# Cross-attention: values weighed for 512 tokens at once, and a group's projection moved into the next group's first half

## The chip, the cores and the metric

The kernel runs on one core of one Trainium2 chip. The metric is device time in microseconds (us) of one execution, taken as the median of several runs. The profile is that of one execution; its times are counted from the first to the last instruction of the core, which is called the span.

## The reference, cut to what matters

A decoder block with causal self-attention, cross-attention and a feed-forward part is followed by a fusion block. There are B = 4 sequences of T = 1024 tokens with C = 512 channels and H = 16 heads of DH = 32. The change is in the cross-attention alone, whose keys and values come from a context of S = 64 positions:

```python
xn2 = _ln(x, g2, be2)
q = einsum('btc,hcd->bhtd', xn2, Wq_c) + bq_c      # likewise k and v, from the context
scores = einsum('bhtd,bhsd->bhts', q, k) / scale
attn = softmax(scores, axis=-1)
ca = einsum('bhts,bhsd->bhtd', attn, v)            # the weighing of the values
x = x + (ca @ W2 + b2)                             # the projection
```

## The kernel before, in words

The kernel has three phases, `self_attention`, `cross_attention` (L973) and `feed_forward` (L1255). Work is written as steps with a cost each, and `run` (L106) weaves several streams of steps together by the shares of their costs that are left. The instructions of one engine are then put into a fixed order when the program is built, by a scheduler that works from the order of writing and from its own estimate of when each instruction can start. On the chip every engine goes through its own list strictly in order.

Cross-attention works on eight groups of 512 tokens (`groups`, two to a sequence). For a group, `self_end` (L1036) makes what comes first: the self-attention's projection (`adds`, tile `po_x`, L1071), its sum with x and the norm, the transposes of the normed tokens (`turn` at L1056, tile `tpn_x`), and the queries (`query` at L1067, tile `pq_x`), which land in the pair of tiles `qT`, a high and a low part. Products that need near full precision are done as three products of such parts; in the profile all of them are on L102, told apart by tile. `cross` (L1087) then does the attention of the group, in eight halves: four blocks `j` of 128 tokens, times two halves of the heads.

- `scores` (L1094): six products of 256 columns into one of two `sc` banks, the least value of each head by VectorE (L1104), then the exponentials. For one half of the heads VectorE subtracts (L1113) and ScalarE does one wide exponential (L1114); for the other ScalarE does eight narrow ones (L1110) straight from the bank. GpSimd multiplies by the inverse sums (L1118).
- `turn` (L1121): four transposes into the one `tp` bank (L1126, tile `tpp_c`), copied by ScalarE to `pT` (L1128), 128 tokens wide.
- `weigh` (L1131): four fp32 products of 64 weight columns by 128 tokens (L1139, tile `av_c`), alternately into the upper and lower 64 partitions. After the second half `split` (L71) cuts the bank into the two parts `ca` (ScalarE L74, VectorE L75).
- `project` (L1153): twelve products of 512 columns (tile `po_c`), the sum with x (L1150), and the store of x to DRAM (L1151).

The order within `cross` is that of L1166: each round writes the scores of one half, the transposes of the half two rounds back and the weighing of the half three rounds back; every second round has the projection of a block whose `ca` is complete. The loop at L1226 runs these steps of group k beside one long stream: the `adds` of group k+2, then the queries of k+1, then the transposes of k+2, with the loads for k+3 strewn in.

Of the eight PSUM banks three belong to `mm` (`po_x`, `tpn_x`, `pq_x`), one to `tp`, two to `av` (`av_c` and `po_c`) and two to `sc`. The x tiles have twelve slots, three groups. A load into a slot waits for the store of the x tile that was there (both on SyncE's queue).

Of the kernel before, what the change touches and what calls it, by code (L numbers as in the profile page):

```python
# [10 lines left out]
F32 = mybir.dt.float32  # L11
FR = mybir.dt.float32r
# [6 lines left out]
P = 128  # L19
B, T, C, H = 4, 1024, 512, 16  # L20
DH = C // H
S = 64
FF = 4 * C
NC = C // P
# [28 lines left out]
def decoder_then_fusion(ctx: ExitStack, tc: tile.TileContext, x, ctxT, cols, rows,  # L53
# [61 lines left out]
    def run(*streams, speed=None, sooner=None):  # L115


        speed = [v for v, s in zip(speed or [1.0] * len(streams), streams) if s]
        sooner = [v for v, s in zip(sooner or [0] * len(streams), streams) if s]
        streams = [s for s in streams if s]  # L120
        left = [sum(t for t, _ in s) or 1 for s in streams]
        total, at = list(left), [0] * len(streams)
        while any(i < len(s) for i, s in zip(at, streams)):
            k = min((k for k in range(len(streams)) if at[k] < len(streams[k])),
                    key=lambda k: (1 - left[k] / total[k]) / speed[k])
            t, f = streams[k][at[k]]
            if sooner[k]:
                with tc.high_priority(offset=sooner[k]):
                    f()
            else:  # L130
                f()
            left[k] -= t
            at[k] += 1

    def behind(*engines):

# [316 lines left out]
    def self_attention(ph):  # L453
# [62 lines left out]
        def front(b, n):  # L516
# [20 lines left out]
                split(parts[0][:, c, :], parts[1][:, c, :], tp, f"{uid}_{c}")  # L537

            return [(0, lambda j=j: load(j)) for j in range(NJ)], [(TG, lambda c=c: turn(c)) for c in range(NC)]

        def among(steps, extra):

            out, n = list(steps), len(extra)
            for i in reversed(range(n)):
                out.insert((i + 1) * len(steps) // (n + 1), extra[i])
            return out

        def tiles_of(b, g):

# [423 lines left out]
    def cross_attention(ph):  # L973
# [27 lines left out]
        ptp = ph.enter_context(tc.tile_pool(name="pt_x", reuse_waits="tile", bufs=3))  # L1001
        big = ph.enter_context(tc.tile_pool(name="big_x", reuse_waits="tile", bufs=1))

        def parts_of(name, uid, bufs=1):
            pool = {"qT": big, "sa": sap, "xn": xnp}[name]
            return [pool.tile([P, NC, TG], FR, tag=f"{name}{k}", name=f"{name}{k}_{uid}", bufs=bufs)
                    for k in range(2)]

        sas, state = {}, {}

        def self_parts(b, n):

            uid = f"x{b}_{n}"

            def begin():
                if b == B - 1:
                    for step in invert_steps(b, n, nc.sync):
                        step()

                sas[b, n] = parts_of("qT", uid, 2) if Z["sa1"] and (b, n) == groups[1] else parts_of("sa", uid)  # L1020

            def divide(g):
                inv = avp.tile([P, TG], F32, tag="inv", name=f"inv_{uid}_{g}")
                src = inv_dram[b, n].rearrange("(g r) t -> g r t", r=HG)
                for r in range(HG):
                    nc.sync.dma_start(inv[r * DH : (r + 1) * DH],
                                      src[g, r : r + 1].to_broadcast([DH, TG]))
                av = avp.tile([P, TG], F32, tag="sav", name=f"sav_{uid}_{g}")
                nc.sync.dma_start(av, av_dram[b, n, g])
                nc.gpsimd.tensor_tensor(av, av, inv, ALU.mult)  # L1030
                sa = sas[b, n]
                split_biased(sa[0][:, g, :], sa[1][:, g, :], av, col("bv_s", g))

            return [(0, begin)] + [(1, lambda g=g: divide(g)) for g in range(NC)]

        def self_end(b, n):  # L1036
# [18 lines left out]

            def turn(c):  # L1056
                if c == 0:
                    held["xn"], held["q"] = parts_of("xn", uid), parts_of("qT", uid, 2)
                    state[b, n] = xs, held["q"]
                xn = held["xn"]  # L1060
                tp = psum(f"tpn_{uid}_{c}")
                for j, t in enumerate(hs):
                    nc.tensor.transpose(tp[:, j * P : (j + 1) * P], t[:, c * P : (c + 1) * P], ident)
                nc.scalar.activation(tp, tp, AF.Identity, bias=col("be2", c), scale=col("g2", c))
                split(xn[0][:, c, :], xn[1][:, c, :], tp, f"{uid}_{c}")

            def query(ps, g):  # L1067
                q = held["q"]
                split_biased(q[0][:, g, :], q[1][:, g, :], ps, nbq[:, NC + g : NC + g + 1])

# [16 lines left out]
        def cross(b, n):  # L1087
# [6 lines left out]
            def scores(j, half):  # L1094
# [9 lines left out]
                nc.vector.tensor_reduce(top, sc, AX.X, ALU.min)  # L1104
                pr = ptp.tile([P, HH, S], F32, tag="p", name=f"p_{uid}")
                den = small.tile([P, HH], F32, tag="denc", name=f"den_{uid}", bufs=2)
                if half:
                    nc.vector.tensor_scalar(top, top, QSCALE, None, ALU.mult)
                    for h in range(HH):
                        nc.scalar.activation(pr[:, h], sc[:, h], AF.Exp, scale=-QSCALE,  # L1110
                                             bias=top[:, h : h + 1], accum_out=den[:, h : h + 1])
                else:
                    nc.vector.tensor_tensor(pr, sc, top.unsqueeze(2).to_broadcast([P, HH, S]), ALU.subtract)  # L1113
                    nc.scalar.activation(pr, pr, AF.Exp, scale=-QSCALE)  # L1114
                    nc.vector.tensor_reduce(den, pr, AX.X, ALU.add)
# [5 lines left out]
            def turn(j, half):  # L1121
                uid = f"c{b}_{n * NJ + j}_{half}"
                pr = held.pop((j, half)).rearrange("p h s -> p (h s)")
                tp = ps_tp.tile([P, TG], F32, tag="tp", name=f"tpp_{uid}")
                for k in range(4):
                    nc.tensor.transpose(tp[:, k * P : (k + 1) * P], pr[:, k * P : (k + 1) * P], ident)  # L1126
                pT = ptp.tile([P, 4, P], F32, tag="pT", name=f"pT_{uid}", bufs=2)
                nc.scalar.copy(pT.rearrange("p k q -> p (k q)"), tp)  # L1128
                held["pT", j, half] = pT

            def weigh(j, half):  # L1131
                uid = f"c{b}_{n * NJ + j}_{half}"
                if half == 0:
                    held["av", j] = ps_av.tile([P, TG], F32, tag="av", name=f"av_{uid}")
                av, pT = held["av", j], held["pT", j, half]
                for k in range(4)[::-1]:
                    m = half * 4 + k
                    r = (m % 2) * 2 * DH
                    nc.tensor.matmul(av[r : r + 2 * DH, (m // 2) * P : (m // 2 + 1) * P],  # L1139
                                     vbd[:, b, m, :], pT[:, k, :], start=True, stop=True)  # L1140
                if half:
                    ca = [ptp.tile([P, NC, P], FR, tag=f"ca{k}", name=f"ca{k}_{uid}", bufs=2)
                          for k in range(2)]
                    flat = [t.rearrange("p c q -> p (c q)") for t in ca]
                    split(flat[0], flat[1], av, uid)
                    held["ca", j] = ca

            def added(ps, j):
                i = n * NJ + j
# [2 lines left out]

            def project(j):  # L1153
                return product_steps(lambda: ps_av.tile([P, C], F32, tag="av", name=f"po_c{b}_{n * NJ + j}"),
                                     lambda: held["ca", j], lambda: w2,
                                     lambda a, c: a[:, c, :], lambda w, c: w[:, c, :], C,
                                     lambda ps: added(ps, j))

            def biased(j):
# [2 lines left out]

            steps = [(0, lambda: load_context(b + 1))] if n == 0 and b < B - 1 else []
            steps += [(0, lambda j=j: biased(j)) for j in range(NJ)]
            halves = [(j, h) for j in range(NJ) for h in range(2)]
            for k in range(len(halves) + 5):  # L1166
                if k < len(halves):
                    steps.append((3 * C, lambda at=halves[k]: scores(*at)))
                if 0 <= k - 2 < len(halves):
                    steps.append((2 * C, lambda at=halves[k - 2]: turn(*at)))  # L1170
                if 0 <= k - 3 < len(halves):
                    steps.append((2 * C, lambda at=halves[k - 3]: weigh(*at)))
                if 0 <= k - 5 and (k - 5) % 2 == 1:
                    steps += project((k - 6) // 2)
            return steps

        ends = [self_end(*at) for at in groups] + [([], [], [], [])] * 3
        run(ends[0][0] + ends[0][1])
# [1 line left out]
        if Z["a2"] >= 3:  # L1180
# [2 lines left out]

        kbd = [[wts.tile([P, NC, HG * S], FR, tag=f"kbd{k}_{i}", name=f"kbd{k}_{i}") for k in range(2)]
               for i in range(2)]
        vbd = wts.tile([P, B, H // 2, 2 * DH], F32, tag="vbd", name="vbd")

        def load_context(b):
            eng = nc.sync if b else nc.scalar
            for k, t in enumerate(kbd[b % 2]):  # L1190
                eng.dma_start(raw(t), kbd_dram[k, b])
            eng.dma_start(vbd[:, b], vbd_dram[:, b])

        gate = ExitStack()
        k = Z["a2k"]
# [25 lines left out]
        else:  # L1221
            load_w2()
            with gate:
                run(ends[2][0])
            run(ends[1][2])
        for k, at in enumerate(groups):  # L1226

            later = list(ends[k + 1][3]) + ends[k + 2][2]
            for i, step in enumerate(ends[k + 3][0]):
                later.insert(2 * i, step)  # L1230
            steps = cross(*at)
            if k == 0 and Z["w2l"]:
                steps.insert(Z["w2l"], (0, load_w2))
            run(steps, ends[k + 2][1] + later, speed=(1.5,1.0))

# [569 lines left out]
```

## Time and profile before

| | |
|---|---|
| median of three runs | 2153.99 us (2148.6 to 2155.89) |
| the profiled execution | 2153.24 us, span 2151.5 us |
| TensorE, VectorE, ScalarE, GpSimd busy | 96%, 67%, 45%, 56% of the span |
| granted TensorE clock, mean | 0.983 |
| cross-attention's scores, first and last start | 959.2 to 1320.0 us |
| its projections, last start | 1341.3 us |

Times in the tables of the profile are busy times of an engine. An engine's next instruction can begin before the last one's recorded end, since the engines overlap the tail of one with the head of the next; where the text speaks of a pitch, it is the time from one start to the next. An fp32 product of this kernel leaves two records, so 256 products of `av_c` are 512 records.

### The profile page before, as it was taken

The numbers are of one execution on the slowest core, as the hardware profiler recorded it, in microseconds if no ns is written. First come the engines' busy times: TensorE is split into PE (matmuls) and PEld (weight loads), VectorE is DVE, ScalarE is ACT, GpSimd is POOL, SyncE is SP. The second block draws the span as 40 slices with busy tenths as digits, with TensorE's granted clock in tenths as the row PEclk, the third lists the DMA queues.
The fourth block names the chain that finished last, engine by engine and source line by source line (L and its number), as shares of the span: only waits on it lengthen the run. The fifth ranks groups of instructions, "written<-read, shape, count | busy, mean of one in ns | idle before, by whom it ended". The sixth has DMA issues, their size and how long they took to land.

```text
span 2151.5 us, 34750 instructions
## 1 busy us (share of the span) xinstructions
PE 2064.3 (96%) x11544; PEld 1568.7 (73%) x11544; DVE 1452.1 (67%) x3134; ACT 967.5 (45%) x2180; POOL 1210.7 (56%) x1257
## 2 busy tenths in 40 slices
PE   6999998999999989989999999999999999999997
PEld 5766676667667756457888887788788888888885
DVE  6587757665755587567676776877667846865667
ACT  3365555555565545435555557433322422232222
POOL 3288878888788877774555543512343524433323
PEclk9999999999999998999999999999999999999998
DMA  8866767677666567662323122965576457655631
GB/s 245 258 186 168 218 203 216 182 243 219 190 174 186 158 171 213 206 204 79 99 84 103 50 79 86 332 210 170 182 238 198 166 175 237 207 175 171 220 113 39
DMA packets 241321, 379.36 MB, mean 176 GB/s; under 512 B 35948, under 2 KB 104284, under 8 KB 239094
## 3 DMA queue, kind: packets, MB, share of 16 engines
q1 hardware_dynamic: 215532, 348.32, 52.4%
q10 hardware_dynamic: 25610, 28.83, 4.4%
q8 instruction: 92, 1.51, 0.3%
q14 instruction: 87, 0.71, 0.1%
HBM read 251.71 MB, written 124.81 MB: 175 GB/s over the span
## 4 chain that ended last, share of the span: by engine, by line
PE 76%; DMA 7%; DVE 7%; POOL 4%; issue 2%; ACT 1%; SPq 1%; ACTq 0%; DVEq 0%; POOLq 0%
PE acc L1495 15%; PE ph L1473 14%; PE st L755 5%; PE s L692 5%; PE av L785 5%; PE po_c L102 4%; PE pq_x L102 3%; PE pk L102 3%; PE pv L102 3%; PE pg_o L102 3%; PE po_x L102 3%; PE pq L102 3%; POOL pT L809 2%; PE sc_c L87 2%; PE av_c L1139 1%
## 5 line engine op out<-in xcount | busy, mean ns | idle before, releaser
L809 POOL TENSOR_TENSOR pT<-pT,pT 128x256 f32<-128x256 f32 (+3 forms) x369 | 551.6, 1514 | 106.0 <-PE av L785 97.1
L760 ACT ACTIVATE pT<-st 128x512 f32<-128x512 f32 (+2 forms) x640 | 322.3, 559 | 171.2 <-PE st L755 122.9
L1495 PE MATMUL acc<-wf,hs 128*128 128x512 f32 x1536 | 392.1, 393 | 0.9 <-DVE y L1507 0.9
L1495 PEld LDWEIGHTS acc<-wf,hs 128*128 128x128 f32 x1536 | 285.8, 188 | 63.1 <-ACT inT L74 1.3
L699 DVE CUSTOM_DVE_ANT_0 s<-s,mask 128x128 f32<-128x128 f32 (+3 forms) x512 | 244.5, 504 | 99.6 <-PE s L692 97.1
L692 PE MATMUL s<-ks,qs 96*128 96x512 f32 (+3 forms) x768 | 230.2, 371 | 23.0 <-DMA qs<-qd 7.3
L702 DVE TENSOR_REDUCE top<-s 128x1 f32<-128x512 f32 x256 | 171.9, 684 | 104.4 <-PE s L692 103.9
L755 PE MATMUL st<-qs,ks 98*128 98x256 f32 (+2 forms) x888 | 227.8, 340 | 4.7 <-ACT pT L760 2.0
L1473 PE MATMUL ph<-inT,wp 128*128 128x512 f32 x768 | 205.3, 396 | 3.1 <-DVE p L1431 1.2
L755 PEld LDWEIGHTS st<-qs,ks 98*128 98x128 f32 x888 | 149.4, 192 | 63.7 <-issue 20.2
L692 PEld LDWEIGHTS s<-ks,qs 96*128 96x128 f32 x768 | 135.6, 194 | 81.0 <-issue 17.0
L1473 PEld LDWEIGHTS ph<-inT,wp 128*128 128x128 f32 x768 | 143.9, 189 | 36.6 <-DVE gp_o L1568 1.8
L785 PE MATMUL av<-pT,v 128*32 128x512 f32 (+3 forms) x1776 | 155.1, 454 | 4.1 <-POOL pT L768 4.1
L1473 PE MATMUL ph<-inX,wp 128*128 128x512 f32 x576 | 151.4, 395 | 1.1 <-DVE inX L75 1.1
L768 POOL TENSOR_SCALAR_AFFINE_SELECT pT<-pT 128x256 f32<-128x256 f32 x256 | 103.7, 421 | 73.6 <-ACT pT L760 73.1
L1473 PEld LDWEIGHTS ph<-inX,wp 128*128 128x128 f32 x576 | 108.4, 189 | 25.2 <-issue 1.3
L1542 POOL TENSOR_TENSOR y<-y,row_bf 128x512 f32<-128x512 f32 x32 | 41.6, 1304 | 132.6 <-DMA y<-x 72.1
L1481 ACT ACTIVATE hs<-ph 128x512 fp32r<-128x512 f32 x64 | 38.3, 599 | 172.2 <-DVE ph L1431 99.4
L102 PE MATMUL pk<-xn_s,wk 128*128 128x512 f32 x384 | 106.1, 412 | 4.9 <-DVE top L702 3.0
L102 PE MATMUL pv<-wv,xn_s 128*128 128x256 f32 x768 | 108.1, 286 | 2.5 <-DVE least L699 1.6
L102 PEld LDWEIGHTS pv<-wv,xn_s 128*128 128x128 f32 x768 | 102.1, 192 | 11.4 <-DVE top L699 2.9
L1118 POOL TENSOR_TENSOR p_c<-p_c,inv_c 128x512 f32<-128x512 f32 x64 | 68.4, 1069 | 73.9 <-DVE inv_c L1117 58.6
(262 smaller groups left out, 3907.8 us busy)
## 6 DMA issues: line engine op xcount, KB each, us to landing
wp<-wpd SPq DMA_DIRECT2D x168, 256.0 KB
ks<-kd SPq DMA_DIRECT2D x96, 256.0 KB
qs<-qd SPq DMA_DIRECT2D x96, 256.0 KB
wf<-w2fd SPq DMA_DIRECT2D x48, 512.0 KB
kd<-k SPq DMA_DIRECT2D x64, 256.0 KB
qd<-q SPq DMA_DIRECT2D x120, 128.0 KB
wpd<-wp SPq DMA_DIRECT2D x56, 256.0 KB
x<-in_x SPq DMA_DIRECT2D x32, 256.0 KB
```

What stands on the lines that cost most here:

```text
L102: nc.tensor.matmul(held["ps"], a_at(a()[i], c), b_at(b()[j], c), start=not bias and c == 0 and k == 0, stop=c == NC - 1 and k == 2)
L692: nc.tensor.matmul(part, q_at[u][:KS, r, j * P : (j + 1) * P], k_at[u, m][:KS, r, : part.shape[-1]], start=True, stop=True)
L699: nc.vector.tensor_tensor_reduce(part, part, mask[:, TG - part.shape[-1] :], 1.0, TOP, ALU.add, ALU.min, dst)
L702: nc.vector.tensor_reduce(dst, part, AX.X, ALU.min)
L755: nc.tensor.matmul(st[:, i], k_at[u, kb // NJ][:KM, r + i, (kb % NJ) * P : (kb % NJ + 1) * P], q_at[u][:KM, r + i, c0:], start=True, stop= ...
L760: nc.scalar.activation(held[kb][(r + i) // 2][:, at : at + k, c0:], st[:, i : i + k], AF.Exp, scale=-QSCALE)
L768: nc.gpsimd.affine_select(out=t, in_=t, compare_op=ALU.is_ge, fill=0.0, base=0, pattern=[[0, 2], [1, P]], channel_multiplier=-1)
L785: return nc.tensor.matmul(held["av"][r * DH : (r + 1) * DH, c0:], v_at[b, g][:, kb, r * DH : (r + 1) * DH], held[kb][r // 2][:, r % 2, c0: ...
L809: eng.tensor_tensor(t[:, :, c0:], t[:, :, c0:], p[:, :, c0:], ALU.add)
L1118: nc.gpsimd.tensor_tensor(pr, pr, inv.unsqueeze(2).to_broadcast([P, HH, S]), ALU.mult)
L1473: nc.tensor.matmul(ps, w[:, q, c], x[:, r, c], start=c == 0 and m == 0, stop=c == HC - 1 and m == 2)
L1495: mm = nc.tensor.matmul(accs[j], hidden[b, n, f][:, q, j * P : (j + 1) * P], w2s[b, f][:, r], start=begins and m == 0, stop=ends and m == 2)
```

## The change

`weigh` is now called once for each of the four blocks `c` of 128 channels, after the scores and transposes of all four token blocks, and weighs 512 tokens at a time: two fp32 products of 64 weight columns by 512 tokens, into one whole `av` bank, which is split at once into channel block `c` of `ca`. So there are 64 products of `av_c` in place of 256. The splits, the copies, the exponentials and the transposes stay as many as they were, and each of the same size; a copy now writes four strips of 128 into a `pT` that is 512 wide.

The halves run over all four token blocks of one half of the heads, then of the other. Which path the exponentials take goes by the token block and no longer by the half. `ca` lies in the room of the group's queries, which the scores have finished with by then. The room is one of two, taken in turn by the groups.

`cross` returns two lists, its own steps and its projection (`sums`). The loop runs the first half of group k's steps, with the projection of group k-1 strewn among them, beside the `adds` of k+2; then the second half beside the queries of k+1, the transposes of k+2 and the loads for k+3. The last group's projection comes at the end by itself. The context's block-diagonal values `vbd` have two buffers in place of one for each sequence.

```diff
-                pT = ptp.tile([P, 4, P], F32, tag="pT", name=f"pT_{uid}", bufs=2)
-                nc.scalar.copy(pT.rearrange("p k q -> p (k q)"), tp)
-                held["pT", j, half] = pT
+                if j == 0:
+                    held["pT", half] = ptp.tile([P, 4, TG], F32, tag="pT", name=f"pT_{uid}", bufs=2)
+                nc.scalar.copy(held["pT", half][:, :, j * P : (j + 1) * P], tp.rearrange("p (k q) -> p k q", k=4))
 
-            def weigh(j, half):
-                uid = f"c{b}_{n * NJ + j}_{half}"
-                if half == 0:
-                    held["av", j] = ps_av.tile([P, TG], F32, tag="av", name=f"av_{uid}")
-                av, pT = held["av", j], held["pT", j, half]
-                for k in range(4)[::-1]:
-                    m = half * 4 + k
-                    r = (m % 2) * 2 * DH
-                    nc.tensor.matmul(av[r : r + 2 * DH, (m // 2) * P : (m // 2 + 1) * P],
-                                     vbd[:, b, m, :], pT[:, k, :], start=True, stop=True)
-                if half:
-                    ca = [ptp.tile([P, NC, P], FR, tag=f"ca{k}", name=f"ca{k}_{uid}", bufs=2)
-                          for k in range(2)]
-                    flat = [t.rearrange("p c q -> p (c q)") for t in ca]
-                    split(flat[0], flat[1], av, uid)
-                    held["ca", j] = ca
+            def weigh(c):
+                if c == 0:
+                    held["ca"] = room_of(b, n, f"ca{b}_{n}")
+                av = ps_av.tile([P, TG], F32, tag="av", name=f"av_c{b}_{n}_{c}")
+                for k in range(2)[::-1]:
+                    m = 2 * c + k
+                    nc.tensor.matmul(av[k * 2 * DH : (k + 1) * 2 * DH], vbd[b][:, m, :],
+                                     held["pT", m // 4][:, m % 4, :], start=True, stop=True)
+                ca = held["ca"]
+                split(ca[0][:, c, :], ca[1][:, c, :], av, f"ca{b}_{n}_{c}")
...
-            halves = [(j, h) for j in range(NJ) for h in range(2)]
-            for k in range(len(halves) + 5):
+            halves = [(j, h) for h in range(2) for j in range(NJ)]
+            for k in range(len(halves) + 2):
                 if k < len(halves):
                     steps.append((3 * C, lambda at=halves[k]: scores(*at)))
                 if 0 <= k - 2 < len(halves):
                     steps.append((2 * C, lambda at=halves[k - 2]: turn(*at)))
-                if 0 <= k - 3 < len(halves):
-                    steps.append((2 * C, lambda at=halves[k - 3]: weigh(*at)))
-                if 0 <= k - 5 and (k - 5) % 2 == 1:
-                    steps += project((k - 6) // 2)
-            return steps
+            steps += [(4 * C, lambda c=c: weigh(c)) for c in range(NC)]
+            sums = []
+            for j in range(NJ):
+                sums += project(j)
+            return steps, sums
...
+        sums = []
         for k, at in enumerate(groups):
-            later = list(ends[k + 1][3]) + ends[k + 2][2]
+            steps, next_sums = cross(*at)
+            half = len(steps) // 2
+            run(among(steps[:half], sums), ends[k + 2][1])
+            ahead = list(ends[k + 1][3]) + ends[k + 2][2]
             for i, step in enumerate(ends[k + 3][0]):
-                later.insert(2 * i, step)
-            steps = cross(*at)
-            if k == 0 and Z["w2l"]:
-                steps.insert(Z["w2l"], (0, load_w2))
-            run(steps, ends[k + 2][1] + later, speed=(1.5,1.0))
+                ahead.insert(2 * i, step)
+            run(steps[half:], ahead)
+            sums = next_sums
+        run(sums)
```

## The prediction, as put on record before the run

> **What bounds the kernel now.** I read the page first, then busy time by stretches of 10 us through cross-attention, then the groups of instructions in that window, then the timeline of single products.
>
> ```profile
> PE 2064.3 (96%) x11544; PEld 1568.7 (73%) x11544; DVE 1452.1 (67%) x3134; ACT 967.5 (45%) x2180; POOL 1210.7 (56%) x1257
> PEclk9999999999999998999999999999999999999998
> ```
>
> TensorE leads, but a share of the whole span says nothing of one stage. The stretches do (columns: time, then busy us of PE, PEld, DVE, ACT, POOL, clock, DMA share, GB/s):
>
> ```profile
> 1060.00:1070.00 10.00, 10.00 (x74) 8.36 (x70) 9.04 (x16) 9.29 (x29) 2.58 (x3) 1.00 0.22 79
> 1070.00:1080.00 10.00, 10.00 (x59) 8.35 (x59) 5.37 (x12) 2.57 (x12) 5.14 (x6) 1.00 0.18 54
> ...
> 1290.00:1300.00 10.00, 8.44 (x67) 6.50 (x64) 10.00 (x22) 7.62 (x33) 2.85 (x3) 1.00 0.47 181
> 1300.00:1310.00 10.00, 10.00 (x67) 8.23 (x66) 5.49 (x13) 7.24 (x34) 2.85 (x3) 1.00 0.17 63
> 1310.00:1320.00 10.00, 9.51 (x74) 7.51 (x73) 7.94 (x16) 6.63 (x31) 3.42 (x4) 1.00 0.13 46
> 1320.00:1330.00 10.00, 8.37 (x54) 6.47 (x53) 3.37 (x9) 6.05 (x29) 3.13 (x3) 1.00 0.08 28
> ...
> 1340.00:1350.00 10.00, 7.25 (x25) 4.88 (x24) 8.62 (x14) 7.06 (x15) 6.50 (x7) 0.76 0.76 244
> ```
>
> From 970 to 1286 us PE has no gap worth naming: there, every product taken away is time saved, so long as nothing else becomes late. From 1286 to 1342, in the last two groups, PE idles 4 of 56 us. So the question is what PE saves, and whether ACT and DVE, nearly full in some stretches already, still serve it in time.
>
> **PE's saving.** The products that change, and their wide neighbour of the same kind (fp32, few weight columns, 512 tokens), in the timeline:
>
> ```profile
> 1042.43 0.27 PE L1126 MATMUL tpp_c<-ident,p_c 128*128 128x128 f32 x1
> 1042.63 0.66 PE L1139 MATMUL av_c<-pT_c,vbd 128*64 128x128 f32 x8
> 1043.22 0.50 PE L102 MATMUL pq_x<-xn_x,wqc 128*128 128x512 f32 x1
> ```
> ```profile
> 506.24 1.06 PE L822 MATMUL den<-pT,ones 128*32 128x512 f32 x8
> 507.24 0.45 PE L755 MATMUL st<-qs,ks 98*128 98x384 f32 x1
> ```
>
> Before, a half takes 1043.22 - 1042.63 = 0.59 us for eight records, in four waves of two side by side (records start 6 ns apart, waves 0.11 to 0.16 apart). Entry costs as well: the last transpose to `av_c` is 0.20 us, where to a weight product it is 0.03, so 0.17 more. That is 0.76 us x 64 halves = 48.6 us. After, a channel block is two waves of 512; the `den` waves start at 506.243 and 506.696, the next product at 507.24, and further waves of this kind follow after 0.43. The instruction order of the changed program puts two blocks together each time: 0.45 + 2 x 0.43 + 0.54 + 0.17 = 2.0 us, 16 times = 32 us. Saving 16.6 us. Bounds: if two 64-column products did not run side by side at 512 tokens, waves would be 8 instead of 4, 16 x 4 x 0.43 = 27 us more, a loss of 11; the pairs 6 ns apart speak against that, and I take 16.6.
>
> Not all of it lies in the dense part. I cut at the end of the last query product (PE row of `pq_x`: last start 1286.3, so 1286.5). Up to there the order has 49 of 64 halves before and 12 of 16 double blocks after: 37.2 - 24.0 = 13.2 us saved; but two halves' scores and transposes (0.72 + 0.36 us each) come in front of the cut now, which are 2.2. So **-11 us at the cut** if PE stays dense.
>
> **What costs nothing.** Copies (64), splits (32 + 32), exponentials and loads are as many and as big; the order shows PE alone with fewer. The `pT` copy writes strips of 128; its row is 0.60 us by element count, bounds 0 to +0.1 us a copy off the path. The room: scores have finished with the queries before `ca` is written, and the next queries for it come after the projection; cover over 10 us each, so 0. `vbd` in two buffers: its load waits for a group finished long before, 0.
>
> The moved projection also moves the store of x, which SyncE's queue must do before the load of x for group k+3, since there are twelve slots. The chain of waits has this once: x sum 0.70, store 2.05, load 2.73, GpSimd's b1 1.04 us, then a sum of 0.69 again: 7.2 us from the end of a projection until a `po_x` bank is free, and loads behind it on SyncE wait as well. With three `mm` banks the fourth `po_x` needs it; in the new order 10.8 us of PE work (three projections and a `po_x`) lie between. Hidden by 3.6 us; if GpSimd and DVE are each two instructions late, the cover is gone and each group pays 0 to 2 us. I take 0.
>
> **The seams.** Before, the transposes `tpn_x` of the next group lie among projections, which have their own two banks. After, the projections are elsewhere, and in each of six seams the order is: scores, `tpp_c`, `tpn_x`, three more scores, three `tpp_c`, with nothing else PE could do until the first `po_x`. ACT's pitch when busy, from its timeline:
>
> ```profile
> 1319.22 0.31 ACT L1110 ACTIVATE p_c<-sc_c,top_c 128x64 f32<-128x64 f32 x1
> 1319.41 0.21 ACT L1110 ACTIVATION_READ_ACCUMULATOR p_c<-sc_c,top_c 128x1 f32 x1
> 1319.51 0.32 ACT L1110 ACTIVATE p_c<-sc_c,top_c 128x64 f32<-128x64 f32 x1
> ```
>
> So eight narrow exponentials take 8 x 0.29 = 2.3 us, not the 4.5 of the busy sums; likewise pitch 0.48 for a `pT` copy or a cast, 0.68 for the `tpn_x` activation, 0.52 for a wide exponential, 0.57 for a query. In the worst seam (first group of the second sequence, second half) PE, after the score that waits for the last narrow exponential, has 0.72 + 0.72 + 0.36 + 0.45 = 2.25 us until `tpp_c` of the fourth block, which needs the bank emptied. ACT's list up to that copy: query 0.57, copy 0.48, two activations 1.36, exponential 0.52, cast 0.48, copy 0.60 = 4.0. PE waits 1.75 us; then the next score waits for a subtraction on DVE queued behind that transpose, 0.35; and the score before came 0.4 late. 2.5 us. Counted the same way the other five give 0.5, 1.0, 1.3, 1.3 and 1.7: 8.3 in all, and 0.3 each for the way from engine to engine: **10 us**. Bounds: 0 (before, PE waits nowhere there) and 27 (with the rows' whole durations in place of pitches the worst seam is 5.3, on average 4.5).
>
> **The end.** From the cut to the last projection, before: 1341.5 - 1286.5 = 55.0 us. After, PE has 43.8 us of work there (9 halves' scores 6.5, 12 sets of transposes 4.3, 4 double blocks 8.0, 8 projections 21.9, feed-forward's transposes 3.1). The last projections wait for the whole group now, four in a row. Followed link by link, ACT's and DVE's lists leave PE waiting 2.1 + 2.9 + 0.9 in the first ten us, then 1.7 and 2.6 around the last scores, and about 3 in engine-to-engine steps: 57, so **+2**. Bounds: 48 (projections cover all but the last softmax) and 62.
>
> **Sum.** 2153.2 - 11 + 10 + 2 = 2154.2 against the profiled execution; that lies 0.8 under the median of the runs shown, so I say 2155.
>
> One rule of the Trainium skill speaks against the change. The row first: after waits in 1340 to 1350, none over 1.6 us, the clock is 0.76, while in 1290 to 1300 and 1320 to 1330, with 1.6 us idle in each, it stays 1.00. "TensorE: Matmul & The Clock Gate", section "What's actually happening", has the clock halve after an idle window of about 3.4 us; by that no seam would trip it, and the sum stays. By the row of 1340 a seam that idles a quarter of its ten us might, and would run some 4 us at half speed, an estimate of 2 us a seam, 12 in all. No row shows which holds for the seams.
>
> **Rivals.**
> *ACT keeps up.* Seams cost nothing, as before 1286 now, and the end is as long as it was: 2153 - 11 = 2142. For it: over a group ACT's pitches sum to some 27 us of 46. Against: 10.5 of them fall within the 10.8 us of PE work of the worst seam.
> *The seams starve PE.* A price of 4 us a seam (24) and an end of 60 (+5): 2153 - 11 + 29 = 2171, slower. For it: PE waits in line order, the single `tp` bank makes each set of transposes wait for ACT, and p has three buffers. It decides from where seams and end together pass 18 us. Against: pitches, not durations, rule ACT in the row above.
> *The pairs do not run side by side:* 2155 + 27 = 2182; little stands for it.
>
> **How the numbers follow.** Gain given back at the seams, time within 0.3% of before (6.5 us, about what a measurement of this kernel can tell from no change): 0.37. ACT keeps up, faster: 0.27. Seams starve PE, slower: 0.33; no pairs: 0.03, slower too. The range reaches down to the second case with a shorter end (2138) and up past 2171 to an end at its bound (2173).
>
> **What would show it.** `av_c` as 128 records in waves of two 0.43 apart; PE waits at `tpp_c`, `sc_c` and `tpn_x` for ACT and DVE, some 10 us in all, in six places between 1000 and 1280; the cut about 1 us earlier than 1286.5; the end some 57 us. Wrong if PE's gaps there stay under 3 us or go over 20, if the clock drops in seams, or if `po_x` is seen waiting for x.

## The result, and the profile after

The changed kernel takes 2165.34 us (median of 6 runs, 2161.41 to 2171.03), the kernel before beside it 2151.84 us (6 runs): a ratio of 1.0063, 95% interval 1.0044 to 1.0082, so 0.6% slower. The forecast was 2155, no measurable change. The time lies inside the stated range of 2138 to 2173, but that range took in the rivals as well. What came is the rival in which the seams starve PE, at a price between its own and the forecast's.

The profiled execution of after is the fastest of the six, 2161.41 us (span 2159.7), only 8.2 above the profiled one of before. The two can't be compared end to end: the first score product starts at 953.1 us after and at 959.2 before, with the same work ahead of it, and over all builds of this study that start lies between 953 and 964. So I measure each trace over the **stage**, from its first `sc_c` to the first product of the feed-forward part (`ph`): 385.0 us before, 398.5 after. These 13.5 us are as many as lie between the medians; with one trace of each kernel, an agreement that close is partly luck.

Busy time and clock row on the page of after:

```profile
PE 2055.0 (95%) x11160; PEld 1549.9 (72%) x11160; DVE 1448.1 (67%) x3134; ACT 964.9 (45%) x2180; POOL 1213.7 (56%) x1257
...
PEclk9999999999999999999999999999999999999999
```

PE is 9 us less busy, with 384 fewer records (192 products), and yet the kernel is slower: PE waits. (The clock row shows nothing: a slice of it is 54 us wide.) The stretches of after (columns as before):

```profile
1060.00:1070.00 10.00, 10.00 (x47) 8.17 (x46) 1.66 (x3) 2.12 (x12) 1.92 (x2) 1.00 0.23 79
...
1090.00:1100.00 10.00, 6.71 (x43) 5.62 (x41) 8.35 (x13) 4.87 (x20) 6.93 (x7) 1.00 0.28 80
1100.00:1110.00 10.00, 9.26 (x48) 7.67 (x50) 6.68 (x15) 9.75 (x31) 2.09 (x2) 0.83 0.00 1
...
1300.00:1310.00 10.00, 7.09 (x26) 3.82 (x27) 6.52 (x17) 4.80 (x21) 3.13 (x3) 0.66 0.41 157
...
1340.00:1350.00 10.00, 10.00 (x46) 8.21 (x45) 5.09 (x8) 1.94 (x4) 4.49 (x5) 1.00 0.39 132
```

Read the first line against the next two. At 1060 PE is full while the softmax engines have little to do (DVE 1.66, ACT 2.12 us): projections run there that need no softmax. At 1090 PE starves, and at 1100 its clock is down as well. What PE waited for within the stage (line, releaser: us in all, times, longest), the first four lines:

```profile
PE sc_c L87 <- ACT p_c L1115: 6.7, 4, 3.5
PE tpn_x L1065 <- DVE q_qx L80: 4.0, 4, 2.1
PE sc_c L87 <- DVE p_c L1118: 4.0, 3, 2.6
PE tpp_c L1131 <- ACT pT_c L1134: 3.0, 4, 1.4
```

All lines of this view come to 24 us; in before they come to 5.8, the first being:

```profile
PE po_c L102 <- DVE ca_c L75: 2.7, 4, 1.4
```

The longest wait stands in the seam I had called the worst, in the first group of the second sequence. On PE's timeline:

```profile
1096.00 0.80 PE L1065 MATMUL tpn_x<-ident,xh_x 128*128 128x128 f32 x3
1100.33 2.34 PE L87 MATMUL sc_c<-kbd,q_qx 128*128 128x256 f32 x12 [3.52 <-ACT p_c L1115]
1102.46 1.06 PE L1131 MATMUL tpp_c<-ident,p_c 128*128 128x128 f32 x4
```

And on the timelines of GpSimd, VectorE and ScalarE, the instructions that lead to it:

```profile
1094.46 0.55 POOL L179 TENSOR_TENSOR rstd_x<-rstd_x,neg_half 128x1 f32<-128x1 f32 x1
1094.98 1.05 POOL L1123 TENSOR_TENSOR p_c<-p_c,inv_c 128x512 f32<-128x512 f32 x1
1096.39 1.27 POOL L1160 TENSOR_TENSOR x_x<-x_x,row_b 128x512 f32<-128x512 f32 x1 [0.36 <-DVE xh_x L185]
```
```profile
1095.05 1.26 DVE L185 TENSOR_SCALAR xh_x<-x_x,mv_x,rstd_x 128x512 f32<-128x512 f32 x1 [1.05 <-POOL rstd_x L179]
1096.23 0.68 DVE L75 TENSOR_TENSOR q_ca<-av_c,q_ca 128x512 fp32r<-128x512 f32 x1
1096.83 0.85 DVE L1113 TENSOR_SCALAR top_c<-top_c 128x8 f32<-128x8 f32 x1
```
```profile
1097.80 0.31 ACT L1115 ACTIVATE p_c<-sc_c,top_c 128x64 f32<-128x64 f32 x1 [4.00 <-DVE top_c L1113]
```

The brackets are read backwards. PE waits for a score bank, which eight narrow exponentials on ACT must empty. ACT stood idle 4.00 us before them, for a scaled maximum on DVE. DVE had that queued behind a normalisation of x, which waited 1.05 us for GpSimd's `rstd`, and behind a split. The exponentials then take their 2.3 us, as I had counted. Two instructions of DVE's list also ran long: the normalisation 1.26 us, where the median of its kind in this trace is 0.55, and the scaled maximum 0.85, where it is 0.17. GpSimd was at work both times, and each ended within 0.3 us after an instruction of GpSimd. The trace of before has about as many long ones, so the change did not bring them, and no run tests why they come. The profile names only the last link of such a chain.

The weighing itself became what was worked out: eight records in 1111.39 - 1109.52 = 1.87 us.

```profile
1109.52 1.94 PE L1143 MATMUL av_c<-pT_c,vbd 128*64 128x512 f32 x8
1111.39 0.66 PE L1131 MATMUL tpp_c<-ident,p_c 128*128 128x128 f32 x4
```

### The profile page after: what moved, and what is told of

Its sections match the earlier page's. It is cut to its first block, busy times and chain, and to the rows that moved or that the text cites. A ratio compares the mean times of both kernels' runs of the same rounds, so it can differ in the third digit from the quotient of the medians.

```text
span 2159.7 us, 33950 instructions
## 1 busy us (share of the span) xinstructions
PE 2055.0 (95%) x11160; PEld 1549.9 (72%) x11160; DVE 1448.1 (67%) x3134; ACT 964.9 (45%) x2180; POOL 1213.7 (56%) x1257
## 3 DMA queue, kind: packets, MB, share of 16 engines
q8 instruction: 89, 1.46, 0.3%
## 4 chain that ended last, share of the span: by engine, by line
PE 73%; DVE 9%; DMA 8%; POOL 4%; ACT 3%; issue 2%; SPq 1%; DVEq 0%; ACTq 0%; POOLq 0%
PE acc L1501 15%; PE ph L1479 14%; PE s L692 5%; PE st L755 5%; PE av L785 5%; PE pk L102 4%; PE pq L102 3%; PE pv L102 3%; PE po_c L102 3%; PE pg_o L102 3%; PE po_x L102 3%; POOL pT L809 2%; PE den L822 1%; PE pq_x L102 1%; PE sc_c L87 1%
```

## The experiments

**Theory.** PE's saving is real. But a group's twelve wide products (four output projections, four self-attention projections, four query products) need nothing of the group's own softmax any more. The planner (the scheduler that fixes each engine's order when the program is built) may spend them early, and what is left of the softmax stands bare. Before, the output projections waited for their own token blocks, so the data itself spread them. **Rivals:** the wide weighing is itself dear; the softmax lists are too long in any order; the end of the stage or the banks are the cause.

"Five groups" below is the time from the 9th to the 49th of the 64 sets of transposes `tpp_c` in the trace. Ratios are to the kernel before as it ran beside each run, with 95% intervals; each kernel is described below. The last two columns come from one trace each, and the five groups hold a slightly different number of records in each order (720 wide ones in paced, 727 in before, 738 in after).

| kernel | ratio | stage, us | five groups, us |
|---|---|---|---|
| before | 1 | 385.0 | 253.0 |
| after | 1.0063 [1.0044, 1.0082] | 398.5 | 262.5 |
| narrow products in after's order | 1.0047 [1.0029, 1.0065] | 395.7 | 263.9 |
| two query products held back | 1.0058 [1.0038, 1.0078] | 395.9 | 267.5 |
| paced | 1.0003 [0.9988, 1.0018] | 385.3 | 243.7 |
| last group in pairs | 1.0072 [1.0053, 1.0091] | 399.7 | 264.5 |
| paced, narrow products | 1.0013 [0.9993, 1.0033] | 391.1 | 245.7 |
| paced, both ends | 1.0006 [0.9989, 1.0023] | 385.6 | 245.1 |
| paced, both ends, pairs | 1.0017 [0.9998, 1.0036] | 384.2 | 245.9 |
| wide exponentials in after | 1.0048 [1.0031, 1.0064] | 393.0 | 260.2 |
| paced, first group | 0.9987 [0.9968, 1.0007] | 380.9 | 246.1 |
| paced, first group, pairs | 0.9993 [0.9973, 1.0013] | 381.4 | 246.3 |
| paced, first group, shifted | 0.9992 [0.9975, 1.0008] | 383.3 | 243.2 |
| three score banks in after | 1.0102 [1.0071, 1.0133] | 400.8 | 262.1 |

**1. Narrow products in after's order.**

```diff
-                for k in range(2)[::-1]:
-                    m = 2 * c + k
-                    nc.tensor.matmul(av[k * 2 * DH : (k + 1) * 2 * DH], vbd[b][:, m, :],
-                                     held["pT", m // 4][:, m % 4, :], start=True, stop=True)
+                for j in range(NJ):
+                    for k in range(2)[::-1]:
+                        m, at = 2 * c + k, slice(j * P, (j + 1) * P)
+                        nc.tensor.matmul(av[k * 2 * DH : (k + 1) * 2 * DH, at], vbd[b][:, m, :],
+                                         held["pT", m // 4][:, m % 4, at], start=True, stop=True)
```

> The changed kernel, but the values are weighed in products of 128 tokens again, at the same places: 512 records of av_c in place of 128, all else as it was. Theory (TensorE's saving is real, and bare softmax stretches without projections eat it): the products cost 0.59 us a half again instead of 0.43 a wave of 512, and up to 0.17 us for each more change of mode, so TensorE has 8 to 17 us more; some of that falls into the bare stretches, where TensorE waits anyway, so the time rises by 5 to 15 us over the changed kernel (2170 to 2180), and against the kernel before the move alone costs 18 to 28 us. Rival 1 (the wide products or the copies and splits around them are themselves what is dear): the time falls back towards the kernel before, 2152 to 2160. Rival 2 (TensorE does not bound cross-attention any more, the softmax lists do throughout): no change, 2163 to 2167.

Measured: 2161.11 us, no slower than after; my 2170 to 2180 was missed, and neither rival's range was met. In the trace the `av_c` products take 14 us more (46.1 in place of 31.9, from start to next start), but PE's gaps up to the last query product fall from 15.7 to 7.0: a narrow product needs only its own token block, so the planner put pieces into the bare stretches. The run doesn't tell the rivals apart; it shows what a filler there is worth.

**2. Two query products held back.** The third and fourth query product of the next group may be issued only behind two transpose sets of this group's second half. With them the transposes of the tokens after are written beside the next group's first half:

```diff
+            for i, (t, f) in enumerate(kept):
+                kept[i] = (t, lambda f=f, at=(1, 2)[i // NC]: after_turn(at, f))
```

> The changed kernel with only the order of issue changed: of the next group's four query products, the third and the fourth are put behind the second and third of a group's last four transpose sets, so that 5.2 us of projection work stands inside each seam; the work is the same. Theory (the seams starve TensorE because the planner has spent all projections before them): the seams' waits of TensorE fall from some 15 us to under 7, and with the clock that drops behind them the time falls by 8 to 15 us (2150 to 2157), unless a new bare stretch forms earlier in the second half, where these products came from; then by 3 to 8. Rival (ActE's and VectorE's lists are as long as the stretch, so what fills TensorE does not shorten it): the time stays within 3 us of 2165 and the waits stand elsewhere.

Measured: 2163.96 us, five groups 267.5. Nothing won: PE's gaps within the five groups are 13.4 us, where after has 11.4. The stall of 3.52 us at 1100 is gone, but others stand elsewhere, 1.71 us at 1051, 2.75 at 1205 and 2.37 at 1261. The time is in the rival's range and misses the theory's, with its "new bare stretch" too (3 to 8 us less). That products taken from one stretch left another bare is my reading, not shown; the next run decides.

**3. Paced.** Every wide product is put behind one of the group's eight transpose sets (c output, x self-attention, q query). The edit fixes the places of the transposes of x, the weighings and the loads as well, so it tests the order as a whole; the work is unchanged:

```diff
+        ORDER = [[('c', 0)], [('c', 1), ('c', 2)], [('c', 3)], [('x', 0), ('q', 0)], [('x', 1)], [('q', 1), ('x', 2)], [('q', 2)], [('x', 3), ('q', 3)]]
...
+                with tc.issue_after(latest["turn", groups[k], i]):
+                    for kind, n in ORDER[i]:
+                        for _, f in product(kind, k, n):
+                            f()
```

> The changed kernel with all twelve wide products of a group (four output projections, four self-attention projections, four query products) put one or two behind each of the group's eight transpose sets, so that none can be issued early; the work is the same. Theory (clustered softmax work without cover costs about 21 us, of which 11 were won by the wide products): cross-attention up to the last query product gets dense as before the change, and the time falls by 12 to 21 us, to 2144 to 2153; the end stays 59 us long. Rival (the softmax lists are too long in any order, or the moved projection's store and load chain holds the next group): the time stays at 2160 to 2168, with TensorE waiting for ACT and DVE or for x as much as now.

Measured: 2151.48 us, 0.6% under after: order alone gives back what the change cost, and its interval lies clear of that of after. Five groups take 243.7 us, 18.8 less than after and 9.3 less than before, and PE has no gap in them. Stretches of this kernel:

```profile
970.00:980.00 10.00, 8.39 (x32) 6.43 (x30) 4.00 (x9) 7.05 (x35) 4.18 (x4) 0.59 0.00 1
1090.00:1100.00 10.00, 10.00 (x55) 8.52 (x54) 5.61 (x13) 5.12 (x21) 4.51 (x7) 1.00 0.01 2
1100.00:1110.00 10.00, 10.00 (x46) 6.40 (x45) 8.49 (x17) 6.17 (x23) 4.43 (x6) 1.00 0.17 53
```

The two lines at 1090 and 1100 stand beside those of after above: PE full, DVE and ACT at an even 5 to 8.5 us. The lists are not too long; they were badly timed. But the line at 970 shows a hole at the start, with the clock at 0.59, where before and after have none, and the end (49th transpose set to `ph`) takes 83.3 us in place of 67.7 before and 78.0 after. Against before nothing is won overall.

**4. The last group in pairs of token blocks.**

```diff
+            halves = [(j, h) for j0 in range(0, NJ, 2 if last else NJ)
+                      for h in range(2) for j in range(j0, j0 + (2 if last else NJ))]
```

> The changed kernel, where the last group alone takes its blocks of 128 tokens in two pairs: both halves of the first pair, its values weighed over 256 tokens, then the second pair, so that the first two of its projections can run beside the second pair's softmax. Theory (the end grew from 55 to 59 us because all four last projections wait for the whole group): the end shrinks by 4 to 8 us to 51 to 55, and the time falls by 4 to 8 us to 2157 to 2161; the seams are untouched. Rival (the end is set by the softmax lists, not by where the projections stand): the end stays within 1.5 us of 59 and the time within 2 us of 2165.

Measured: 2167.06 us; from the last query product to the last projection 57.6 us in place of 59.4. The rival holds, to within 0.1 us of its bound on the time: the end is not set by where the projections stand alone.

**5. Paced, narrow products** (the edits of 3 and 1 together).

> The paced order, with the values weighed in products of 128 tokens again (512 records of av_c). Theory (TensorE's saving is real and worth its full size where projections cover the softmax; in the first run with narrow products it was hidden, since the narrow products of a token block can start earlier and filled the bare stretches): here, where TensorE has no gaps over five groups, the time rises by 8 to 17 us over the paced kernel (2151.5), to 2160 to 2168, and five groups take 5 to 10 us more than its 243.7. Rival (wide products save nothing, because something beside TensorE paces the groups): within 3 us of 2151.5.

Measured: 2152.77 us, five groups 2.0 us longer. The time is in the rival's range, but not for the rival's reason: nothing beside TensorE paces the groups, whose gaps are 0.4 us here. My size was off as well, and this is the most useful miss. The two kernels' `av_c`, narrow first:

```profile
1098.20 1.53 PE L1145 MATMUL av_c<-pT_c,vbd 128*64 128x128 f32 x24
1099.66 0.66 PE L1131 MATMUL tpp_c<-ident,p_c 128*128 128x128 f32 x4
```
```profile
1086.56 1.94 PE L1144 MATMUL av_c<-pT_c,vbd 128*64 128x512 f32 x8
1088.43 0.86 PE L87 MATMUL sc_c<-kbd,q_qx 128*128 128x256 f32 x5
```

Twenty-four narrow records take 1.46 us, which makes 1.95 for 32. Where 32 stand in one run, three times in this trace, they take 1.90. Eight wide ones, the same work, take 1.87. So in one unbroken run the width is worth 0.03 to 0.08 us a double block, 0.5 to 1.3 us in all. But the planner breaks the narrow ones up: `av_c` stands in 65 runs in before, 42 here and 20 in paced. With what each entry costs beyond the usual pitch, PE spends 48.9, 40.7 and 34.3 us on it. So 8.2 of the 14.6 us that paced saves come without the width, from many token blocks weighed in one go with fewer entries from other kinds of product. The other 6.4 come with the wide product, mostly because it can't be broken up. (The profiled execution took 2165.27 us, 12.5 above this kernel's median, with a lowered clock at the start; its stage is not to be leaned on.)

**6 and 7. Both ends, without and with pairs.** The first two self-attention projections ahead of the first transposes, and other lists for the first and the last two groups (those of run 6; run 7 has two of the last group's own projections in `LAST`):

```diff
+        FIRST = [[('x', 2)], [('x', 3)], [('q', 0)], [('q', 1)], [], [('q', 2)], [], [('q', 3)]]
+        SIXTH = [[('c', 0)], [('c', 1)], [('c', 2)], [('c', 3)], [('q', 0)], [('q', 1)], [('q', 2)], [('q', 3)]]
+        LAST = [[('c', 0)], [], [('c', 1)], [], [('c', 2)], [], [('c', 3)], []]
```

> The paced order, and beside it other orders for the first and the last two groups, where the pacing left TensorE without work: in the first group the first two self-attention projections come ahead of the first transposes, in the seventh one product goes behind each transpose set, in the last the four projections of the group before go behind every other set. Theory (what the paced kernel lacks against a gain is at its two ends: 7 us of idle time and a clock of 0.74 to 0.91 between 950 and 990, and some 8 us of idle time from 1250 on): the hole at the start goes and the time falls by 6 to 12 us under the paced kernel, to 2140 to 2146, faster than the kernel before. Rival (the start and the end cost the same in any order, because the first and the last softmax have nothing to hide behind): 2149 to 2154.

> As the run before, and the last group in two pairs of token blocks (values weighed over 256 tokens), so that two of its own projections run beside the second pair's softmax. Theory (the last projections waiting for the whole group cost some 4 us at the end): 2 to 6 us under the run before. Rival (ACT and DVE set the end; in the changed kernel's own order the pairs gained nothing): within 2 us of it.

Measured: 2153.09 and 2153.80 us. The rivals hold. The start (first score to 9th transpose set) went from 58.3 to 49.9 and 48.6 us as expected, and the end from 83.3 to 90.6 and 89.7: given back. The largest wait there in the kernel without pairs:

```profile
1266.85 2.49 PE L87 MATMUL sc_c<-kbd,q_qx 128*128 128x256 f32 x12 [3.84 <-ACT p_c L1115]
```

One filler a set, spread thin where the seventh group begins, makes a seam of the same kind again; with the old lists there, run 9 has an end of 84.8.

**8. Wide exponentials in after.**

```diff
-                if j % 2:
+                if False:
```

> The changed kernel, with the exponentials of every block taken in the wide form (subtraction on VectorE, one activation of 512, a sum on VectorE), where it takes every other block in eight narrow activations on ScalarE. ScalarE has 1.8 us less for each of 32 blocks, VectorE some 0.5 to 1 us more. Theory A (in the bare stretches TensorE waits for ScalarE's list, the narrow exponentials above all, as my prediction's seam count has it): the waits of sc_c for the narrow exponentials go and the time falls by 4 to 10 us, to 2155 to 2161. Theory B (the narrow exponentials only stand at the end of a chain that begins on VectorE and GpSimd: the maximum waits behind a normalisation that waits for GpSimd's rstd): the waits move to VectorE and the time stays or rises, 2164 to 2175.

Measured: 2163.42 us, between the ranges of the two theories and, within the intervals, not to be told from after. With an estimated 32 x 1.8 us taken off ACT, the waits for the narrow exponentials (6.7 us) go, and those for DVE's subtraction rise from 4.0 to 7.0. The first line now reads:

```profile
PE sc_c L87 <- DVE p_c L1118: 7.0, 7, 2.2
```

So ScalarE's list, on which my seam count rested, is not the main cause. In the trace the stage is 5.5 us shorter, so it may have a part.

**9 to 11. First group only; the same with pairs; the first with the last query product shifted into the next group** (the first two with FIRST as in 6, the second with the last group's blocks in pairs as in 4; for the third, `ORDER` and FIRST are changed so that q3 stands behind the next group's first set, and the transposes of x stand one set later).

> The paced order with only the first group's order changed as in the run with both ends (two self-attention projections ahead of the first transposes, then one product behind a set); the last two groups are as in the paced kernel. Theory (in the run with both ends, the start took 49.9 us in place of 58.3 for the same work, and the end lost as much again, 90.6 in place of 83.3, since one product a set left a bare stretch of 3.8 us where the seventh group begins): start and end are separate, so the time falls by 5 to 9 us under the paced kernel, to 2143 to 2147, faster than the kernel before. Rival (whatever is won early is lost again at the end, because the last softmax of the chain has a time of its own): 2150 to 2154.

> As the run before, and the last group in two pairs of token blocks, with the projections of the group before behind its first four transpose sets and two of its own behind the sixth and seventh. Theory (projections at the end wait for the whole group): 2 to 5 us under the run before, 2139 to 2144. Rival (the pairs did nothing in the changed kernel's order, and 0.7 us more in this one): within 2 us of it.

> The paced order, the first group as in the two runs before, and in every group the last query product moved from behind the eighth transpose set to behind the first of the next group, and the transposes of the next tokens one set later, so that each group's beginning (two scores, two weighings, four transposes of x) has a product of its own to cover it. Theory (bare stretches cost wherever they stand, and the paced kernel's and its successor's last one stands where the seventh group begins): the stall of 3.8 us there goes, 2 to 5 us under the run with only the first group changed. Rival (the list of VectorE is full in that stretch, 10.0 of 10 us, so that a product only moves the wait): within 2 us of it.

Measured: 2151.07, 2151.01 and 2151.47 us, ratios 0.9987, 0.9993 and 0.9992. All three are in their rivals' ranges. The stage of the first is 380.9 us, 4.4 under paced and 4.1 under before, less than the 5 to 9 expected, and in the medians it is not to be told from either: of 8.3 us won at the start, 3.9 are lost further on. Pairs and shift add nothing. No version of this study is shown to be faster than the kernel before.

**12. Three score banks in after** (two in place of three for `po_x`, `pq_x` and `tpn_x`).

```diff
-        ps_mm = ph.enter_context(tc.tile_pool(name="ps_mm_x", reuse_waits="tile", bufs=3, space=PSUM))
+        ps_mm = ph.enter_context(tc.tile_pool(name="ps_mm_x", reuse_waits="tile", bufs=2, space=PSUM))
...
-        ps_sc = ph.enter_context(tc.tile_pool(name="ps_sc_x", reuse_waits="tile", bufs=2, space=PSUM))
+        ps_sc = ph.enter_context(tc.tile_pool(name="ps_sc_x", reuse_waits="tile", bufs=3, space=PSUM))
```

> The changed kernel with three PSUM banks for scores in place of two, and two in place of three for the products before the softmax (po_x, pq_x and the transposes of x). Most of what TensorE waits for in the changed kernel are score banks: sc_c for the narrow exponentials 6.7 us, for the subtraction 4.0, for the maximum 1.7. Theory A (ScalarE's and VectorE's lists in the bare stretches are long, and a bank more only lets TensorE run 0.72 us further ahead once in each stretch): 0 to 5 us less, 2160 to 2165, or more time if the two other banks become short. Theory B (the bound is the two banks, not the lists): the 12 us of sc_c waits go and the time falls by 8 us or more, under 2157.

Measured: ratio 1.0102, with an interval that overlaps that of after. PE's waits at `sc_c` fall from 12.4 to 5.4 us, and others take their place, the first two lines being:

```profile
PE av_c L1143 <- ACT pT_c L1134: 4.5, 5, 1.4
PE ph L1479 <- DVE t L1413: 3.6, 1, 3.6
```

The stage is 2.3 us longer, and the feed-forward part 5.2 (from `ph` to PE's last product 799.3 in place of 794.1), which the planner orders anew as well. Up to the last projection the stage is 1.3 us shorter. So the 12 us of theory B do not come; but the run also took a bank from three other tiles, so what a score bank alone is worth it does not show.

## Why the prediction held in its range and missed in its middle

- **What bounds the kernel:** right. PE sets the pace; a product taken away is time saved where PE is dense (run 3).
- **PE's saving, 16.6 us:** near in size. On `av_c` and its entries PE spends 48.9 us before (48.6 in the forecast) and 34.1 after (32), so 14.8 are saved. Five eighths of the forecast are 10.4; paced has 9.3 in five groups, of which some 0.9 is the other mix of records. The side-by-side pairs hold too. But I credited the 512 columns with it, and by run 5 over half comes from weighing in one go.
- **What costs nothing:** right. No `po_x` waits for x, and the room and `vbd` cost nothing visible.
- **The seams, +10 us: the step that failed.** From the first score to the last query product the trace went from 327.0 to 337.2 us, where -11 + 10 stood. With the saving as predicted, the price is some 21 us. PE's gaps in this part rose from 1.7 to 15.7 us; the clock, below, adds up to 3.4; 2 to 4 us I can't assign. The places were right, even the worst one, but not the chain: I followed ACT's list up to the `pT` copy, as if every other engine delivered in time. The `pT` copy is 1.2 us of the waits in this part, score banks are 7.5 and the splits of the queries 4.0. In the seams at 1100, 1152 and 1204 ACT stood idle for 4.00, 2.27 and 2.48 us for a scaled maximum of DVE, whose list had itself waited 1.05, 0.72 and 0.43 us for GpSimd's `rstd`. At 998, where PE waited 2.09 us for a split, ACT's own list stood before it, as I had counted. I had also assumed a calm clock; that it drops in seams was one of my signs of being wrong, and in two it did.
- **The end, 57 us:** 59.4. Direction right, 2.4 too little; a score at 1303.5 waited 2.62 us for a subtraction on DVE, and the clock in 1300 to 1310 is 0.66. The step from the last projection to `ph` became 1.1 us shorter. In sum 10.2 + 4.4 - 1.1 = 13.5, the loss. That the time is still inside the range is due to its width, not to the price of the seams.
- **The clock rule of the Trainium skill** ("TensorE: Matmul & The Clock Gate", "What's actually happening"): by it no seam as I had counted them would trip the gate. The trace of after, in stretches of 2 us:

```profile
998.00:1000.00 2.00, 0.21 (x2) 0.21 (x3) 2.00 (x4) 2.00 (x5) 0.18 (x1) 1.00 0.05 17
1000.00:1002.00 2.00, 1.80 (x16) 1.59 (x15) 2.00 (x5) 2.00 (x6) 0.00 (x0) 1.00 0.00 0
...
1102.00:1104.00 2.00, 2.00 (x12) 1.97 (x10) 1.53 (x5) 2.00 (x4) 0.00 (x0) 0.50 0.00 0
...
1204.00:1206.00 2.00, 0.97 (x6) 0.77 (x6) 1.18 (x3) 2.00 (x7) 1.04 (x1) 1.00 0.00 0
1206.00:1208.00 2.00, 1.56 (x8) 1.16 (x8) 2.00 (x4) 2.00 (x5) 0.00 (x0) 0.72 0.00 0
1208.00:1210.00 2.00, 1.69 (x8) 1.72 (x9) 1.56 (x5) 2.00 (x5) 0.00 (x0) 0.50 0.00 0
```

The gap of 3.52 us before 1100 is of the rule's size (about 3.4 us), and the clock falls to 0.50 after it: there the two agree, as they do at 1000, where it stays at 1.00 after a gap of 2.09. But at 1206 the clock halves although PE's longest gap there was 0.89 us. Two of six seams tripped it (1100 and 1206) and the end once (1302, after gaps of 1.42 and 2.62 us). Summing the missing clock over the 2 us stretches gives at most 1.7, 1.7 and 3.4 us. So neither fits: the row's 2 us for a seam that pays are near, but only two pay, and one of them not by the rule.

- **The rivals:** "The seams starve PE" was to decide from 18 us of seams and end together, and they came to some 25 (21 + 4.4). It had 29, and 2171. I gave it 0.33, though the single chain that I had walked through could not exclude it.

**What stays open.** Records at their usual pitch (0.232 us a wide product, 0.120 a score, 0.088 a transpose, `av_c` by its own time) add up, by my estimate, to 361 us of the stage before and 351 in after, paced and run 9 alike. What lies beyond (idle time, entries, the lowered clock) is, at the start, in five groups and at the end: 6.1, 10.7 and 7.0 us before; 8.4, 23.0 and 16.3 after; 8.2, 7.6 and 14.1 in run 9. So the ten us saved are there, and in the best order 7 of them go at the end. I read that as the whole group that must be through its softmax before its four projections start; no run shows it, and the pairs, which should have mended it, did not. No run moves `rstd` off GpSimd, so the chain at 1100 is read from the trace, not shown by an experiment (the trace of run 4, the same order up to the last group, has the same stall of 3.52 us); that the order as a whole is the cause is shown by run 3.

## What to carry to other kernels

When an edit frees work from a dependence, ask what that dependence was pacing: filler that may run at any time is spent at the first chance, and latency-bound work then stands bare. Before pricing a bare stretch, follow the lists of all engines, not just of the one that releases PE, since each may stand behind another's wait. And many small products of one kind can be worth nearly as much as one wide product (1.90 against 1.87 us here), so long as nothing is put between them.

## What the hardware showed that I had not expected

PE's clock fell to 0.50 after partial idleness (0.97 us busy in 2 us, no gap over 0.89) and stayed at 1.00 after a single gap of 2.09 us, so in this trace neither the longest gap nor the idle share of two us tells whether a seam will pay. Grouped products of 128 columns cost 0.061 us a record in their waves, against 0.074 where eight stand alone between other products. And the start of the stage wandered by 11 us between builds with the same work ahead of it, more than the effect measured here, which is why a stage within the trace was a better ruler than the span.
